# A graph attention layer on one core: prologue loads moved to another queue, more buffers, a score table split in seven

## The chip, the cores and the metric

The kernel runs on one core of one Trainium2 chip. The metric is the device time of one execution in microseconds: 4080.77 in the median of three runs (4079.7 to 4087.65). The profile shown is of one further execution, of 4080.57 us, whose span (from the first to the last profiled instruction) is 4078.8 us.

A core has five engines that run their own instruction streams in order and wait for one another through semaphores: TensorE (PE), VectorE (DVE), ScalarE (ACT), GpSimd (POOL) and SyncE (SP). Data is moved by DMAs, which in this kernel are issued from the streams of SP, ACT and POOL. An engine that waits holds up everything that stands behind the waiting instruction in its own stream.

## The reference

Nodes x (12500 x 64), 400000 edges with a source, a destination and 64 features each; the edges come sorted by destination. For every edge a score is made from its source row, its destination row and its features, a softmax is taken over the edges of one destination, and the weighted source rows and features are summed per destination.

```python
h_src = nfeats[src]
h_dst = nfeats[dst]
z_att = concatenate([h_src, h_dst, efeats])
e = leaky_relu(z_att @ W_attn + b_attn, 0.01)
m = concatenate([h_src, efeats]) @ W_ne
ex = exp(e - segment_max(e, dst)[dst])
alpha = ex / segment_sum(ex, dst)[dst]
z = segment_sum(alpha * m, dst)
out = relu(concatenate([nfeats, z]) @ W_out)
return layernorm(x + out)
```

## The kernel before

**Tiling.** The sorted edges are cut into 782 groups of 512 (128 partitions with four edges each). Groups are handled in chunks of 24 (`sizes`: 32 chunks of 24, then 10, then 4), and inside a chunk in quads of four groups (`SG`). A quad has two buffers: `ze` for its edge features, loaded by one DMA of 512 KB on SP (L143), and `zx` for its source rows, filled by 16 indirect gathers on POOL (L152), one for each group and place. There are ten `ze` and ten `zx` buffers (`ZB`). The indices of a gather are a column of `srcs`.

**Indices.** `indices` (L102) loads a chunk's indices in natural order (`raw`, SP), turns them into floats (`nat`, ACT, L115), transposes them with eight matmuls into `pp` (L118), and casts the sources back to integers (`srcs`, DVE, L121). There is one `raw`, one `nat` and one `pp`, and there are three `srcs`. `slots_of` (L124) makes from the destinations in `pp` and from `d0b`, each group's first destination on all partitions, the relative destinations `drel`.

**Scores.** `scores` (L158) handles one quad: it loads four rows of `wins` (the destination part of the score for the 48 nodes that begin at a group's first destination) on SP, spreads them over the partitions by a matmul (L163), and makes the scores in VectorE from `ze`, `zx` and these rows (L167 to L186). In chunk 0 the gathers read `x` itself and the source part of the score is computed from the rows (L171, L173); in all later chunks they read `table`, which holds x with the source score as a 65th column.

**Softmax and aggregation.** After a chunk's six quads `softmax` (L226) scans the scores of the whole chunk, and `aggregate` (L322) weights them and sums with matmuls (L333) into `pg` and by VectorE into `acc` (L343). A `zx` or `ze` buffer comes free when the matmuls of its quad have read it; only then may POOL and SP fill it for the quad ten further on. `softmax` also needs the neighbouring destinations, `d3`, loaded on SP by `neighbours` (L205).

**The prologue.** Ahead of the loop, the main body (from L357) does the following.
- It converts the first indices and loads `d0i` (every 512th destination, in one row), `d0p` (the same destinations down the partitions, one element per descriptor), the weights `attn`, `b_col`, `wne`, `wout`, all but the indices on ACT's queue.
- It gathers the first quad from x (`ahead`), and makes `d0b` by three matmuls.
- In 14 blocks of seven times 128 nodes it loads x (`xt`, ACT's queue, three buffers, L395), multiplies and sums on VectorE to make each node's source score (into the 65th column of `xt`) and destination score (`sd`; L400 and L403, each twice), and writes the block to `table` (L404, ACT's queue).
- It transposes `sd`, stores it in DRAM as `sdflat` (L412), and lets one DMA on SP copy it 12544 times, shifted by one node each time, into `shifted` (L419).
- Seven indirect gathers on POOL (`wk`, L423, two buffers) pick the rows of `shifted` at the groups' first destinations, and ACT's queue stores each to `wins` (L426). Between `sdflat` and `shifted`, the gathers of the second to fifth quad are written down.

**What sets the order.** The order in which the text names instructions is not the order in which they run: a scheduler places the instructions of each engine by estimated times, and inserts the semaphore waits. Memory pools also give an order: `pre`, which holds `xt`, `prod`, `wk` and others, is closed after the `wk` loop, and `work`, `rows` and `tiny`, opened after it, reuse its memory; their tiles wait for the readers and writers of what stood there. The two clearings of `worst` and `acc` (L430, L431) stand after it and depend on nothing.

Of the kernel before, what the change touches and what calls it, by code (L numbers as in the profile page):

```python
# [9 lines left out]
F32 = mybir.dt.float32  # L10
I32 = mybir.dt.int32
AF = mybir.ActivationFunctionType
# [3 lines left out]
P = 128  # L16
T = 4
GE = P * T
# [7 lines left out]
S = 48  # L26
# [4 lines left out]
EW = 65  # L31
# [8 lines left out]
def sorted_path(ctx, tc, x, dst, idx, edge, w_ne, w_attn, b_attn, w_out, out, flag):  # L40
# [6 lines left out]
    nc = tc.nc  # L47
    N, D = x.shape
    E = edge.shape[0]
    NB = (N + P - 1) // P  # L50
    NFULL = N // P
# [30 lines left out]
    early = dram.tile([NB * P, D], F32, name="early")  # L82
    sdflat = dram.tile([NB * P + S], F32, name="sdflat")
    shifted = dram.tile([NB * P, S], F32, name="shifted")
    wins = dram.tile([NG, S], F32, name="wins")
    d0i = const.tile([1, NG], I32, name="d0i")
    d0b = const.tile([P, NG], F32, name="d0b")
    worst = const.tile([P, 2], F32, name="worst")
# [9 lines left out]
    w_src = fixed[:, S + D:S + 2 * D].unsqueeze(1)  # L98
    alpha = fixed[:, S + 2 * D:S + 2 * D + T * BG].rearrange("p (t g) -> p t g", t=T)
    win = fixed[:, S + 2 * D + T * BG:S + 2 * D + T * BG + SG * S].rearrange("p (g s) -> p g s", g=SG)  # L100

    def indices(g0, G):  # L102

        raw = chunks.tile([BG, P * 2 * T], I32, name="raw", bufs=1)
        if g0 + G < NG:
            nc.sync.dma_start(out=raw[0:G], in_=idx[g0:g0 + G].rearrange("g p c -> g (p c)"))
        else:

            nc.vector.memset(raw, 0)
            if G > 1:  # L110
                nc.sync.dma_start(out=raw[0:G - 1], in_=idx[g0:g0 + G - 1].rearrange("g p c -> g (p c)"))
            nc.sync.dma_start(out=raw[G - 1:G, 0:RP * 2 * T],
                              in_=idx[NG - 1:NG, P - RP:P].rearrange("g p c -> g (p c)"))
        nat = chunks.tile([BG, P * 2 * T], F32, name="nat", bufs=1)
        nc.scalar.activation(nat[0:G], raw[0:G], AF.Copy)  # L115
        pp = psum.tile([P, 2 * T, BG], F32, name="pp", bufs=1)
        for c in range(2 * T):
            nc.tensor.transpose(pp[:, c, 0:G], nat[0:G].rearrange("g (p c) -> g c p", c=2 * T)[:, c, :],  # L118
                                ident[0:G, 0:G])
        srcs = chunks.tile([P, T, BG], I32, name="srcs", bufs=3)  # L120
        nc.vector.tensor_copy(srcs[:, :, 0:G], pp[:, 0:T, 0:G])  # L121
        return srcs, pp

    def slots_of(g0, G, pp):  # L124
# [33 lines left out]
    def scores(g0, n, ze, zx, drel, b0, y, plain):  # L158

        b = g0 - b0  # L160
        wrow = tiny.tile([1, SG, S], F32, name="wrow")
        nc.sync.dma_start(out=wrow[:, 0:n, :], in_=wins[g0:g0 + n, :].unsqueeze(0))
        nc.tensor.matmul(win[:, 0:n, :], ones_row, wrow[:, 0:n, :], start=True, stop=True)  # L163

        yb = y[:, :, b:b + n].rearrange("p t g -> p g t")
        prod = work.tile([P, SG, T, D], F32, name="prod", bufs=1)
        nc.vector.tensor_tensor(prod[:, 0:n], ze[:, 0:n],  # L167
                                w_edge.unsqueeze(1).to_broadcast([P, n, T, D]), op=OP.mult)
# [182 lines left out]
    while left > 0:  # L351
# [3 lines left out]


    prepared = {0: indices(0, sizes[0])}  # L357
    nc.scalar.dma_start(out=d0i, in_=dst.rearrange("(o n) -> o n", o=1)[:, 0:E:GE])
    NW = (NG + P - 1) // P
    d0p = const.tile([P, NW], I32, name="d0p")  # L360
    nc.vector.memset(d0p, 0)
    nc.scalar.dma_start(out=d0p[:, 0:NW - 1], in_=dst[0:(NW - 1) * P * GE].rearrange("(k p e) -> p k e", p=P, e=GE)[:, :, 0])
    nc.scalar.dma_start(out=d0p[0:NG - (NW - 1) * P, NW - 1:NW],
                        in_=dst[(NW - 1) * P * GE:E].rearrange("(e o) -> e o", o=1)[0:E - (NW - 1) * P * GE:GE, :])
    nc.scalar.dma_start(out=attn, in_=w_attn.rearrange("k o -> o k").to_broadcast([P, 3 * D]))
    nc.scalar.dma_start(out=b_col, in_=b_attn.unsqueeze(0).to_broadcast([P, 1]))
    nc.scalar.dma_start(out=wne[0:D, :], in_=w_ne[D:2 * D, :])
    nc.scalar.dma_start(out=wne[D:2 * D, :], in_=w_ne[0:D, :])
    nc.scalar.dma_start(out=wout, in_=w_out.rearrange("(h k) o -> k h o", h=2))
    ahead = [gather(0, min(SG, sizes[0]), prepared[0][0], 0, True)]  # L370


    sd = const.tile([P, NB], F32, name="sd")
    CB = 7
    nc.scalar.activation(fixed[:, 0:S], slots0, AF.Copy)
    nc.scalar.activation(fixed[:, S:S + D], attn[:, 2 * D:3 * D], AF.Copy)
    nc.scalar.activation(fixed[:, S + D:S + 2 * D], attn[:, 0:D], AF.Copy)
    with tc.tile_pool(name="pre", bufs=2) as pre:
        d0f = pre.tile([1, NG], F32, name="d0f", bufs=1)
        nc.vector.tensor_copy(d0f, d0i)  # L380
        for g0 in range(0, NG, 3 * P):
            n = min(3 * P, NG - g0)
            pb = psum.tile([P, 3, P], F32, name="sm").rearrange("p k n -> p (k n)")
            nc.tensor.matmul(pb[:, :n], ones_row, d0f[:, g0:g0 + n], start=True, stop=True)
            nc.scalar.activation(d0b[:, g0:g0 + n], pb[:, :n], AF.Copy)
        for c0 in range(0, NB, CB):
            c1 = min(c0 + CB, NB)
            f1 = min(c1, NFULL)
            n = c1 - c0
            xt = pre.tile([P, CB, EW], F32, name="xt", bufs=3)  # L390
            if c1 > NFULL:
                nc.vector.memset(xt[:, NFULL - c0:NB - c0, :], 0.0)
                nc.scalar.dma_start(out=xt[0:TAIL, NFULL - c0, 0:D], in_=x[NFULL * P:N, :])
            if f1 > c0:
                nc.scalar.dma_start(  # L395
                    out=xt[:, 0:f1 - c0, 0:D],
                    in_=x[c0 * P:f1 * P, :].rearrange("(b p) f -> p b f", p=P))
            for k, to in ((0, xt[:, 0:n, D]), (1, sd[:, c0:c1])):
                prod = pre.tile([P, CB, D], F32, name="prod")
                nc.vector.tensor_tensor(  # L400
# [3 lines left out]
            nc.scalar.dma_start(  # L404
                out=table[c0 * P:c1 * P, :].rearrange("(b p) f -> p b f", p=P),
                in_=xt[:, 0:n, :])
        nc.vector.tensor_scalar(sd, sd, b_col, None, op0=OP.add)
        psd = psum.tile([P, 3, P], F32, name="sm")[0:NB, 0, :]
        nc.tensor.transpose(psd, sd, ident)
        sdt = pre.tile([NB, P], F32, name="sdt", bufs=1)  # L410
        nc.vector.tensor_copy(sdt, psd)
        nc.scalar.dma_start(out=sdflat[0:NB * P].rearrange("(b p) -> b p", p=P), in_=sdt)  # L412
        zero = pre.tile([1, S], F32, name="zero", bufs=1)
        nc.vector.memset(zero, 0.0)
        nc.scalar.dma_start(out=sdflat[NB * P:NB * P + S].unsqueeze(0), in_=zero)
        while len(ahead) < 5 and (len(ahead) + 1) * SG <= sizes[0]:
            ahead.append(gather(len(ahead) * SG, SG, prepared[0][0], 0, True))
        over = sdflat[0:1]
        nc.sync.dma_start(out=shifted, in_=bass.AP(over.tensor, over.offset, [[1, NB * P], [1, S]]))  # L419
        for k in range(NW):  # L420
            m = min(P, NG - k * P)
            wk = pre.tile([P, S], F32, name="wk")
            nc.gpsimd.indirect_dma_start(  # L423
                out=wk, out_offset=None, in_=shifted[:, :],
                in_offset=bass.IndirectOffsetOnAxis(ap=d0p[:, k:k + 1], axis=0))
            nc.scalar.dma_start(out=wins[k * P:k * P + m, :], in_=wk[0:m])  # L426
    work = loop.enter_context(tc.tile_pool(name="work", bufs=2))
    rows = loop.enter_context(tc.tile_pool(name="rows", bufs=1))
    tiny = loop.enter_context(tc.tile_pool(name="tiny", bufs=2))
    nc.vector.memset(worst, 0.0)  # L430
    nc.vector.memset(acc, 0.0)  # L431

    def own_part(c0):

# [572 lines left out]
```

## Time and profile before

| what | value |
|---|---|
| median of three runs | 4080.77 us |
| the profiled execution | 4080.57 us |
| its span | 4078.8 us |
| POOL busy | 2967.8 us (73%), 3142 instructions |
| VectorE busy | 1875.2 us (46%) |
| TensorE matmul busy | 985.2 us (24%) |
| ScalarE busy | 131.6 us (3%) |
| DMA traffic | 239.80 MB, mean 59 GB/s |

Busy is the time in which an engine ran a profiled instruction; issuing a DMA from SP or ACT is not counted as busy, but it occupies that engine's stream, and the timeline lists it (SPq, ACTq).[...] "issue" names idle time of an engine that waited for nothing the profile shows. An average over the whole span hides stages: here the prologue of some 190 us, with nearly no TensorE work, stands ahead of a long regular stretch, and an end of about 100 us follows it. Granted TensorE clock was 1.00 in the first 200 us and 0.55 to 0.60 from 300 to 4000 us.

### The profile page before, as it was taken

Reading aid. Unit: us, or ns where it says so; the run is one execution under the profiler, and the core shown is the slowest. Engines: PE = TensorE matmul, PEld = TensorE weight load, DVE = VectorE, ACT = ScalarE, POOL = GpSimd, SP = SyncE. Lnnn points to the kernel's source line nnn. Section 1 sums busy time; section 2 is a strip of 40 time slices with the busy share of each in tenths; the row PEclk is TensorE's granted clock in tenths of the full one; section 3 lists DMA queues with packets and bytes.
Section 4 is the critical chain, followed back from the end, with each engine's and each line's share of the span. In section 5 each row is a group of like instructions: output and inputs, shape, how many; then the busy total and the mean of one; then the engine's idle time right before and its main releaser. Section 6 shows DMA issues by size and latency. Waiting matters only on the chain.

```text
span 4078.8 us, 40728 instructions
## 1 busy us (share of the span) xinstructions
PE 985.2 (24%) x14494; PEld 766.8 (19%) x14494; DVE 1875.2 (46%) x4448; ACT 131.6 (3%) x287; POOL 2967.8 (73%) x3142
## 2 busy tenths in 40 slices
PE   0022332132222112222212222211222221122235
PEld 0022322122212011111101111211111120111225
DVE  4174443343555443455444355544335544434656
ACT  0000000000000000000000000000000000000001
POOL 6757777777777777777777777777777777777770
PEclk9985665565555555555555555555555555555555
DMA  8122332232222122222212222212222221222214
GB/s 169 29 51 60 75 75 57 46 74 60 60 60 60 28 59 59 59 60 60 48 39 59 59 60 59 60 34 54 59 60 60 60 59 27 59 58 58 55 26 96
DMA packets 315275, 239.80 MB, mean 59 GB/s; under 512 B 160574, under 2 KB 264233, under 8 KB 315062
## 3 DMA queue, kind: packets, MB, share of 16 engines
q0 software_dynamic: 100320, 104.42, 15.6%
q1 hardware_dynamic: 147462, 116.22, 9.6%
q10 hardware_dynamic: 67280, 16.45, 2.0%
q8 instruction: 117, 1.92, 0.2%
q14 instruction: 96, 0.79, 0.1%
HBM read 226.99 MB, written 12.28 MB: 59 GB/s over the span
## 4 chain that ended last, share of the span: by engine, by line
POOL 41%; DVE 22%; issue 17%; PE 11%; DMA 7%; ACT 1%; DVEq 0%; POOLq 0%; ACTq 0%
POOL zx L152 41%; DMA zx<-table,srcs 7%; PE pg L333 5%; DVE prod L167 3%; DVE y L169 3%; DVE prod L181 3%; PE fixed L163 2%; DVE hot L176 2%; PE sm L200 2%; PE sm L192 2%; DVE acc L343 1%; DVE sdst L184 1%; DVE by_row L197 1%; DVE b L273 1%; DVE w L325 1%
## 5 line engine op out<-in xcount | busy, mean ns | idle before, releaser
L152 POOL DMA_INDIRECT zx<-table,srcs x3032 | 2866.8, 946 | 956.7 <-issue 869.6
L163 PE MATMUL fixed<-wrow,ones_row 1*128 1x192 f32 x392 | 179.0, 553 | 2391.3 <-DVE prod L181 2314.5
L121 DVE CAST srcs<-pp 128x96 int32<-128x96 f32 (+2 forms) x34 | 8.6, 253 | 1587.0 <-DMA zx<-table,srcs 1521.5
L163 PEld LDWEIGHTS fixed<-wrow,ones_row 1*128 1x128 f32 x392 | 88.8, 280 | 2464.9 <-DVE prod L181 2385.1
L333 PE MATMUL pg<-w,ze 128*64 128x48 f32 x6256 | 459.3, 244 | 84.3 <-DVE w L325 73.4
L333 PEld LDWEIGHTS pg<-w,ze 128*64 128x64 f32 x6256 | 449.7, 161 | 104.5 <-DVE w L325 90.1
L333 PE MATMUL pg<-w,zx 128*64 128x48 f32 x6256 | 459.5, 244 | 5.3 <-issue 5.0
L333 PEld LDWEIGHTS pg<-w,zx 128*64 128x64 f32 x6256 | 449.7, 161 | 6.0 <-issue 6.0
L167 DVE TENSOR_TENSOR prod<-ze,fixed 128x1024 f32<-128x1024 f32 x196 | 237.6, 1212 | 86.4 <-DMA wins<-wk 49.9
L169 DVE TENSOR_REDUCE y<-prod 128x16 f32<-128x1024 f32 x196 | 237.2, 1210 | 0.0
L343 DVE TENSOR_TENSOR acc<-acc,pg 128x48 f32 x782 | 158.6, 203 | 164.1 <-PE pg L333 112.9
L325 DVE TENSOR_TENSOR w<-hot,fixed 128x768 f32<-128x768 bf16 x196 | 176.8, 944 | 42.9 <-PE pg L333 37.7
L184 DVE TENSOR_REDUCE sdst<-prod 128x16 f32<-128x768 f32 x196 | 186.1, 950 | 5.1
L181 DVE TENSOR_TENSOR prod<-hot,fixed 128x768 f32<-128x768 bf16 x196 | 185.5, 947 | 0.9
L176 DVE TENSOR_TENSOR hot<-fixed,drel 128x768 bf16<-128x768 f32 x196 | 185.9, 948 | 0.0
L115 ACT ACTIVATE nat<-raw 24x1024 f32<-24x1024 int32 (+2 forms) x34 | 35.9, 1056 | 2876.9 <-PE pp L118 2848.2
L152 POOL DMA_INDIRECT zx<-in_x_dram,srcs x96 | 93.5, 974 | 44.2 <-issue 28.7
L200 PE MATMUL sm<-ones_row,by_row 1*128 1x1 f32 x272 | 79.0, 357 | 108.9 <-DVE by_row L197 75.2
L200 PEld LDWEIGHTS sm<-ones_row,by_row 1*128 1x128 f32 x272 | 67.5, 307 | 176.8 <-DVE by_row L197 138.0
L192 PE MATMUL sm<-order,s 128*1 128x128 f32 x136 | 39.8, 396 | 194.6 <-DVE s L258 112.0
L118 PE MATMUL pp<-ident,nat 24*128 24x24 f32 (+2 forms) x272 | 36.3, 279 | 144.2 <-DVE drel L127 111.4
L174 DVE TENSOR_TENSOR y<-y,zx 128x16 f32<-128x16 f32 x196 | 37.0, 189 | 67.5 <-DMA zx<-table,srcs 64.4
(133 smaller groups left out, 1109.2 us busy)
## 6 DMA issues: line engine op xcount, KB each, us to landing
ze<-in_edge_dram SPq DMA_DIRECT2D x194, 512.0 KB
zx<-table,srcs POOLq DMA_INDIRECT x3032
table<-xt ACTq DMA_DIRECT2D x14, 227.5 KB
wrow<-wins SPq DMA_DIRECT2D x195, 0.8 KB
raw<-in_idx_dram SPq DMA_DIRECT2D x32, 96.0 KB
xb<-in_x_dram ACTq DMA_DIRECT2D x24, 128.0 KB
early<-xo ACTq DMA_DIRECT2D x24, 128.0 KB
xb<-in_x_dram ACTq DMA_DIRECT2D x12, 256.0 KB
```

What stands on the lines that cost most here:

```text
L152: nc.gpsimd.indirect_dma_start(out=zx[:, g, t, 0:D] if plain else zx[:, g, t, :], out_offset=None, in_=x[:, :] if plain else table[:, :], ...
L163: nc.tensor.matmul(win[:, 0:n, :], ones_row, wrow[:, 0:n, :], start=True, stop=True)
L167: nc.vector.tensor_tensor(prod[:, 0:n], ze[:, 0:n], w_edge.unsqueeze(1).to_broadcast([P, n, T, D]), op=OP.mult)
L169: nc.vector.tensor_reduce(yb, prod[:, 0:n], axis=AX.X, op=OP.add)
L176: nc.vector.tensor_tensor(hot[:, 0:n], slots.unsqueeze(1).unsqueeze(1).to_broadcast([P, n, T, S]), drel[:, :, b:b + n].rearrange("p t g -> ...
L181: nc.vector.tensor_tensor(at[:, 0:n], hot[:, 0:n], win[:, 0:n].unsqueeze(2).to_broadcast([P, n, T, S]), op=OP.mult)
L184: nc.vector.tensor_reduce(sdst[:, 0:n], at[:, 0:n], axis=AX.X, op=OP.add)
L192: nc.tensor.matmul(p[0:1, :], col, order, start=True, stop=True)
L200: nc.tensor.matmul(p[:, 0:1], by_row, ones_row[:, 0:1], start=True, stop=True)
L325: nc.vector.tensor_tensor(w[:, 0:n], hot[:, 0:n], alpha[:, :, b:b + n].rearrange("p t g -> p g t").unsqueeze(3).to_broadcast([P, n, T, S]) ...
L333: nc.tensor.matmul(pg[at:at + D, g, :], z[:, g, t, 0:D], w[:, g, t, :], start=(t == 0), stop=(t == T - 1))
L343: nc.vector.tensor_tensor(ag, ag, pg[:, g, :], op=OP.add)
```

## The change

All of it is in the prologue.
- `wins` becomes seven DRAM tiles of 128 rows, and the row loads in `scores` pick the tile. `wk` gets seven buffers.
- `attn`, `d0i`, `b_col`, `d0p`, `wne`, `wout` and x are loaded on SP instead of ACT. `d0i` and `b_col` stand after the first x block; `d0p`, `wne` and `wout` are moved down to the place just ahead of `shifted`.
- x gets 14 buffers, and all its loads are written ahead of the compute blocks and of the first gather.
- Everything in the block that computes `table` and `sd` is to be issued after the first cast of sources (`casts[0]`), by `tc.issue_after`; the clearing of `acc` after the copy of the transposed scores (`casts[1]`).
- `d0b` is made after the fourth block of x rather than ahead of the first.

In the order that the scheduler gives the changed kernel, POOL runs 80 gathers from x, then the seven `wk` gathers, then the other 16 gathers from x, then all of those from `table`. ACT's stream begins with the conversion of the first indices. SP's stream begins with the index load, then `attn`, x, `d0i`, `b_col` and the other x blocks, then the first `ze`.

```diff
-    wins = dram.tile([NG, S], F32, name="wins")
+    wins = [dram.tile([P, S], F32, name=f"wins{k}") for k in range((NG + P - 1) // P)]
...
-        nc.vector.tensor_copy(srcs[:, :, 0:G], pp[:, 0:T, 0:G])
+        cast = nc.vector.tensor_copy(srcs[:, :, 0:G], pp[:, 0:T, 0:G])
+        if not casts:
+            casts.append(cast.ins)
...
-        nc.sync.dma_start(out=wrow[:, 0:n, :], in_=wins[g0:g0 + n, :].unsqueeze(0))
+        for k in range(g0 // P, (g0 + n - 1) // P + 1):
+            a, b1 = max(g0, k * P), min(g0 + n, (k + 1) * P)
+            nc.sync.dma_start(out=wrow[:, a - g0:b1 - g0, :], in_=wins[k][a - k * P:b1 - k * P, :].unsqueeze(0))
...
-    nc.scalar.dma_start(out=d0i, in_=dst.rearrange("(o n) -> o n", o=1)[:, 0:E:GE])
...
-    nc.scalar.dma_start(out=d0p[:, 0:NW - 1], in_=dst[0:(NW - 1) * P * GE].rearrange("(k p e) -> p k e", p=P, e=GE)[:, :, 0])
...
-    nc.scalar.dma_start(out=attn, in_=w_attn.rearrange("k o -> o k").to_broadcast([P, 3 * D]))
-    nc.scalar.dma_start(out=b_col, in_=b_attn.unsqueeze(0).to_broadcast([P, 1]))
...
+    nc.sync.dma_start(out=attn, in_=w_attn.rearrange("k o -> o k").to_broadcast([P, 3 * D]))
+    CB = 7
+    before = ExitStack()
+    pre = before.enter_context(tc.tile_pool(name="pre", bufs=2))
+    xts = []
+    for c0 in range(0, NB, CB):
+        c1 = min(c0 + CB, NB)
+        f1 = min(c1, NFULL)
+        xt = pre.tile([P, CB, EW], F32, name="xt", bufs=(NB + CB - 1) // CB)
...
+            nc.sync.dma_start(
+                out=xt[:, 0:f1 - c0, 0:D],
+                in_=x[c0 * P:f1 * P, :].rearrange("(b p) f -> p b f", p=P))
+        xts.append(xt)
+        if c0 == 0:
+            nc.sync.dma_start(out=d0i, in_=dst.rearrange("(o n) -> o n", o=1)[:, 0:E:GE])
+            nc.sync.dma_start(out=b_col, in_=b_attn.unsqueeze(0).to_broadcast([P, 1]))
...
+    with before:
+
+        before.enter_context(tc.issue_after(casts[0]))
...
-            xt = pre.tile([P, CB, EW], F32, name="xt", bufs=3)
...
+            xt = xts[c0 // CB]
...
+            if c0 == 3 * CB:
+                d0f = pre.tile([1, NG], F32, name="d0f", bufs=1)
+                nc.vector.tensor_copy(d0f, d0i)
...
-        nc.vector.tensor_copy(sdt, psd)
+        casts.append(nc.vector.tensor_copy(sdt, psd).ins)
...
+        d0p = pre.tile([P, NW], I32, name="d0p", bufs=1)
...
+        nc.sync.dma_start(out=d0p[:, 0:NW - 1], in_=dst[0:(NW - 1) * P * GE].rearrange("(k p e) -> p k e", p=P, e=GE)[:, :, 0])
...
+        nc.sync.dma_start(out=wout, in_=w_out.rearrange("(h k) o -> k h o", h=2))
         over = sdflat[0:1]
         nc.sync.dma_start(out=shifted, in_=bass.AP(over.tensor, over.offset, [[1, NB * P], [1, S]]))
...
-            wk = pre.tile([P, S], F32, name="wk")
+            wk = pre.tile([P, S], F32, name="wk", bufs=NW)
...
-            nc.scalar.dma_start(out=wins[k * P:k * P + m, :], in_=wk[0:m])
+            nc.scalar.dma_start(out=wins[k][0:m, :], in_=wk[0:m])
...
-    nc.vector.memset(acc, 0.0)
+    with tc.issue_after(casts[1]):
+        nc.vector.memset(acc, 0.0)
```

More of the change, by code (lines that the diff above doesn't have):

```diff
@@ L100, in sorted_path @@
     win = fixed[:, S + 2 * D + T * BG:S + 2 * D + T * BG + SG * S].rearrange("p (g s) -> p g s", g=SG)
+    casts = []
     def indices(g0, G):
@@ L357, in sorted_path @@
     prepared = {0: indices(0, sizes[0])}
-    nc.scalar.dma_start(out=d0i, in_=dst.rearrange("(o n) -> o n", o=1)[:, 0:E:GE])
[L359 to L364, printed above, removed]
-    nc.scalar.dma_start(out=attn, in_=w_attn.rearrange("k o -> o k").to_broadcast([P, 3 * D]))
-    nc.scalar.dma_start(out=b_col, in_=b_attn.unsqueeze(0).to_broadcast([P, 1]))
-    nc.scalar.dma_start(out=wne[0:D, :], in_=w_ne[D:2 * D, :])
-    nc.scalar.dma_start(out=wne[D:2 * D, :], in_=w_ne[0:D, :])
-    nc.scalar.dma_start(out=wout, in_=w_out.rearrange("(h k) o -> k h o", h=2))
+    nc.sync.dma_start(out=attn, in_=w_attn.rearrange("k o -> o k").to_broadcast([P, 3 * D]))
[7 more added lines that the diff above has]
+        xt = pre.tile([P, CB, EW], F32, name="xt", bufs=(NB + CB - 1) // CB)
+        if c1 > NFULL:
+            nc.vector.memset(xt[:, NFULL - c0:NB - c0, :], 0.0)
+            nc.sync.dma_start(out=xt[0:TAIL, NFULL - c0, 0:D], in_=x[NFULL * P:N, :])
+        if f1 > c0:
+            nc.sync.dma_start(
[5 more added lines that the diff above has]
+            nc.sync.dma_start(out=b_col, in_=b_attn.unsqueeze(0).to_broadcast([P, 1]))
     ahead = [gather(0, min(SG, sizes[0]), prepared[0][0], 0, True)]
     sd = const.tile([P, NB], F32, name="sd")
-    CB = 7
     nc.scalar.activation(fixed[:, 0:S], slots0, AF.Copy)
@@ L377, in sorted_path @@
     nc.scalar.activation(fixed[:, S + D:S + 2 * D], attn[:, 0:D], AF.Copy)
[L378 to L385, printed above, removed]
+    with before:
+        before.enter_context(tc.issue_after(casts[0]))
         for c0 in range(0, NB, CB):
             c1 = min(c0 + CB, NB)
-            f1 = min(c1, NFULL)
             n = c1 - c0
-            xt = pre.tile([P, CB, EW], F32, name="xt", bufs=3)
[L391 to L397, printed above, removed]
+            xt = xts[c0 // CB]
             for k, to in ((0, xt[:, 0:n, D]), (1, sd[:, c0:c1])):
@@ L406, in sorted_path @@
                 in_=xt[:, 0:n, :])
+            if c0 == 3 * CB:
+                d0f = pre.tile([1, NG], F32, name="d0f", bufs=1)
+                nc.vector.tensor_copy(d0f, d0i)
+                for g0 in range(0, NG, 3 * P):
+                    n = min(3 * P, NG - g0)
+                    pb = psum.tile([P, 3, P], F32, name="sm").rearrange("p k n -> p (k n)")
+                    nc.tensor.matmul(pb[:, :n], ones_row, d0f[:, g0:g0 + n], start=True, stop=True)
+                    nc.scalar.activation(d0b[:, g0:g0 + n], pb[:, :n], AF.Copy)
         nc.vector.tensor_scalar(sd, sd, b_col, None, op0=OP.add)
@@ L417, in sorted_path @@
             ahead.append(gather(len(ahead) * SG, SG, prepared[0][0], 0, True))
+        NW = (NG + P - 1) // P
+        d0p = pre.tile([P, NW], I32, name="d0p", bufs=1)
+        nc.vector.memset(d0p, 0)
+        nc.sync.dma_start(out=d0p[:, 0:NW - 1], in_=dst[0:(NW - 1) * P * GE].rearrange("(k p e) -> p k e", p=P, e=GE)[:, :, 0])
+        nc.sync.dma_start(out=d0p[0:NG - (NW - 1) * P, NW - 1:NW],
+                          in_=dst[(NW - 1) * P * GE:E].rearrange("(e o) -> e o", o=1)[0:E - (NW - 1) * P * GE:GE, :])
+        nc.sync.dma_start(out=wne[0:D, :], in_=w_ne[D:2 * D, :])
+        nc.sync.dma_start(out=wne[D:2 * D, :], in_=w_ne[0:D, :])
+        nc.sync.dma_start(out=wout, in_=w_out.rearrange("(h k) o -> k h o", h=2))
         over = sdflat[0:1]
```

## The prediction

> **What bounds the kernel now.** I read the busy row first (POOL 73%, DVE 46%, nobody near full), then the chain that ended last (POOL 41%, "issue" 17%), then POOL's own waits, then the timeline of the first 270 us. The first two say that POOL leads, and the waits say what keeps it from working.
>
> ```profile
> L152 POOL DMA_INDIRECT zx<-table,srcs x3032 | 2866.8, 946 | 956.7 <-issue 869.6
> ...
> POOL zx L152 <- issue: 898.3, 2947, 0.3
> POOL zx L152 <- DMA zx<-table,srcs: 33.2, 109, 0.3
> POOL zx L152 <- PE pg L333: 33.2, 2, 32.9
> POOL zx L152 <- DVE srcs L121: 15.2, 1, 15.2
> ```
>
> An indirect gather takes 0.946 us and 0.30 us of issue stand ahead of it each time, so the pace is one per 1.25 us whatever the rest does (2967 steps from 260.67 to 3970.51). There are 96 + 3032 + 7 = 3135 of them: 3919 of 4078.8 us. Only two waits of POOL are longer than 0.3 us: 15.20 us ahead of the first gather and 32.86 us once, for TensorE's aggregation. A change that makes neither shorter is worth nothing; the prologue matters because both lie in it.
>
> ```profile
> 2.15 7.13 ACTq L362 DMA_DIRECT2D d0p<-in_dst_dram  x1
> 3.71 10.52 DVE L431 MEMSET acc<- 128x12548 f32 x1 [2.56 <-issue]
> ...
> 12.55 1.28 ACT L115 ACT_TABLE_LOAD   x1 [12.55 <-DMA d0i<-in_dst_dram]
> ...
> 13.85 1.06 ACT L115 ACTIVATE nat<-raw 24x1024 f32<-24x1024 int32 x1
> ...
> 16.13 0.26 DVE L121 CAST srcs<-pp 128x96 int32<-128x96 f32 x1 [1.77 <-PE pp L118]
> ...
> 16.67 1.15 POOL L152 DMA_INDIRECT zx<-in_x_dram,srcs  x1 [15.20 <-DVE srcs L121]
> ```
>
> This timeline (start us, duration us, engine) shows why the first gather starts at 16.67. ScalarE converts the first indices (L115) only after it has issued six loads, one of which occupies its queue for 7.13 us; VectorE is in the clearing of acc until 14.23. Both end within half a microsecond of each other, so either alone would have held the start. The indices themselves were there long before: bytes of the stretches 1 to 2, 2.0 to 2.2 and 2.2 to 2.4 us (49, 82 and 164 GB/s) add up to 98 KB, which is the whole 24 x 1024 x 4 byte load, and 2.4 to 2.6 moves nothing.
>
> ```profile
> 148.22 0.94 POOL L423 DMA_INDIRECT wk<-shifted,d0p  x1 [0.30 <-issue]
> ...
> 185.68 0.94 POOL L423 DMA_INDIRECT wk<-shifted,d0p  x1 [0.30 <-issue]
> ...
> 191.19 1.22 DVE L167 TENSOR_TENSOR prod<-ze,fixed 128x1024 f32<-128x1024 f32 x1 [49.94 <-DMA wins<-wk]
> ```
>
> ```profile
> 226.87 0.95 POOL L152 DMA_INDIRECT zx<-table,srcs  x1 [0.30 <-issue]
> 260.67 0.94 POOL L152 DMA_INDIRECT zx<-table,srcs  x1 [32.86 <-PE pg L333]
> ```
>
> These are the other wait's cause. Scores (L167) begin at 191.19, after the last of seven wk gathers (185.68) has landed and been stored in wins: prod lies in a pool that reuses the memory of `pre`, where wk stands. From 191.19 it takes 69.5 us to the point where aggregation has read the first of the ten zx buffers (260.67). POOL has filled all ten by 227.8 and stands for 32.86 us. After that it never stands again until its last gather at 3970.51; 107.3 us of tail follow that one's end.
>
> **The change, part by part.**
>
> *First gather.* The ScalarE queue now issues no load before L118 (formerly L115), and acc's clearing waits for the scores' transposed copy (casts[1]). Remaining chain: index load, landed a little after 2.4; I take 2.8 (0.4 for its completion). The table load (1.28, from 0.82) is over at 2.1. Then the same steps as before, 16.67 - 13.85 = 2.82 us from ACTIVATE to gather. First gather at **5.6**. Ends: 2.4 + 2.8 = 5.2; and, if the load shared the DMA engines as the second index load did (issued 14.93, ScalarE waited for it until 20.40: 5.5 us), 0.8 + 5.5 + 2.8 = 9.1. It stands first on SP as it did before, so the row of the first load is nearer. Gain 16.67 - 5.6 = 11.1 us.
>
> A rule speaks against this part. The Trainium skill, "DMA: Bandwidth & Descriptors", section "Issuing engines are not separate DMA queues", says that all issuers share the same 16 DMA engines and that a choice of issuer saves only the issuing time, usually small. Read so, moving loads from ACT to SP gives about nothing and the time would be 4048. The rows above show the issuing time itself as 11.7 us (0.82 to 12.55) in front of a ScalarE instruction that everything waits for. I go by the row; the rule's other half I accept: the bytes before shifted take as long as they did.
>
> *The seven wk gathers.* In the built order of before, POOL runs 96 gathers from x, then 7 from table, 2 wk, 8, 2 wk, 8, 2 wk, 8, 1 wk: the last wk is number 134. After: 80 from x, 7 wk in one run (seven buffers instead of two), 16 from x, then table; the last is number 87. 47 places of 1.25 us are 58.7 us, plus 11.1 of the start: 185.68 - 69.8 = **115.9**. Scores follow 5.5 us later as before (185.68 to 191.19): 121.4. The seven wins tiles by themselves I cost at nothing: before, the first wins row was multiplied (L163) at 153.43, with five wk still to be gathered, so a whole-tile wait was not there to remove.
>
> *The stall.* From scores to release took 69.5 us. Into that stretch now come the neighbour loads and their VectorE work (d3, far, pf and so on, done earlier in before): some fifteen instructions of 0.06 to 0.29, say 3 us, and a wait of 0 to 3 us for the loads, which wait for the same memory. VectorE's cast of the fourth srcs stands behind two score blocks and needs chunk 0's last x gather: 103 gathers end at 5.6 + 103 x 1.28 = 137.4, landed about 140 (2.45); VectorE gets there at 121.4 + 2 x 7.93 + 5 = 142. No wait. Release at 121.4 + 69.5 + 6 = **197**. POOL needs the buffer after 160 + 7 gathers: 5.6 + 167 x 1.25 + 3.0 (the first 96 ran at 1.28 each, 16.67 to 139.5, which I keep) = 217. Twenty microseconds of cover, so 32.56 us (32.86 less the usual 0.30) go. If the cover fails, each microsecond past 217 costs one. Later buffers come free 2.5 us apart and are wanted 20 us apart.
>
> *SP's queue.* Ahead of shifted it now issues 14 x loads and the tail (0.38 and 0.49 each), attn, b_col, d0i (1.29), d0p (7.13 + 0.92), wne twice, wout, and before them all ten ze: about 18 us of added issuing, plus two index loads that wait for ScalarE conversions, and the semaphore waits[...]. What waits behind is shifted, and behind shifted the first wk, on which POOL would stand in order. Work until shifted has landed: The DMA engines are the limit here (busy share 0.7 to 1.2 in nearly every 5 us from 15 to 75). ACT's queue spent 2.0% of the span, 82 us of all 16 engines, on 67280 packets, so the 12,500 rows of x and the 12,544 of table cost 15 us each; ze's 5.2 MB at the 303 GB/s of 5 to 10 us cost 17; shifted took 18 (issued 80.23, traffic falls away at 99); gathers alone, 100 to 140 us, hold a share of 0.14. Laid end to end from 2.5 us: 65 / 0.86 + 2.5 = 78. VectorE needs 14 x 2.12 = 30 us and is done near 40. The d0p issue of 8 us stands in series on SP with the rest of it, and the scores' column (sdflat) waits for conversions 2 and 3: I add up to 15. Shifted lands at 78 to 93; the first wk is due at 5.6 + 80 x 1.28 = **108**. No cost; below 108 it buys nothing either.
>
> *acc's clearing* now runs beside gathers, about 50 to 65 us, hidden by VectorE's wait for wins until 121. The row gives 10.52 us; The Trainium skill, "VectorE: DVE Perf Modes", section "Zero memsets can be issued as uint32 (trn2)", gives one cycle per element, an estimate of 12548 / 0.96 GHz = 13.07 us. The unexplained 2.56 us ahead of the row make up the difference; I take 13.1. What matters is whether it blocks POOL: "SBUF — State Buffer", section "SBUF: two separate sides", warns that a two-port VectorE operation locks GpSimd out of writing gather descriptors. By that, +10.5 to 13.1 us: 4047 to 4050. The nearest row is the memset of d (128x130) at 61.00, inside the gather of 60.55, which took its usual 0.94. I go by the row: 0.
>
> *Nothing else.* Fourteen x buffers remove VectorE's waits for xt (21.1 us in eleven waits) but those lay under POOL's gathers. The order on PE, VectorE and SP from the second or third chunk on is otherwise as it was, and the tail follows POOL.
>
> **Sum.** Against the profiled execution (4080.57, span 4078.8, so 1.77 around it): 4078.8 - 11.1 - 32.6 = 4035.1; + 1.8 = **4037**. The median shown, 4080.77, lies 0.2 above that execution, which is inside the rounding. That is 1.07% less. Its own range is 4033 (start at 5.2, no slow gathers) to 4042 (start at 9.1, a late microsecond or two).
>
> **Rivals.**
> 1. *The stall stays, smaller.* If scores, the neighbour loads or softmax come more than 20 us later than worked out, POOL stands at its 168th gather. With 30 us more: 4047; with none of the stall gone: 4069.5. For: much of what VectorE, SP and ScalarE do in 121 to 145 is newly packed there. Against: the sum of new work is 6 us.
> 2. *POOL stands at the first wk: the slower side.* Before, wk had 49 us of cover (landed 99, wanted 148); after, 15 to 30. From 108 on each microsecond of shifted or d0p costs one, as all later gathers queue behind it in order. Landing at 120 gives 4049; from 152 on the change loses, and at 165, 4037 + 57 = 4094. For: SP now carries a 7.13 us load issue and two ScalarE-dependent loads ahead of shifted, and the scores' path passes through index conversion 2 and 3. Against: even all of it in series is near 105.
> 3. *The start does not move* (indices land late behind nothing that the trace shows, or the first conversion waits for another load): 4048.
> 4. *The clearing locks POOL*: 4047 to 4050.
>
> **Chances.** Forecast 0.74; stall partly or wholly kept 0.09; POOL at wk with shifted landing below 144, 0.05, from 144 to 160, 0.02, later, 0.04; start unmoved 0.02; lock 0.04. What this kernel's measurement can tell from no change I take as 0.2%, 8 us: that is rival 2 with a landing of 144 to 160 (0.02). Only a later one is slower (0.04); all else is faster (0.94). The range leaves out those 0.06, half of rival 1 and the long end of the 0.05 at the top, and a microsecond under my own low end covers the bottom: 4032 to 4050.
>
> **What would show it.** First gather near 5.6; no wait of POOL over 1 us after it, and none at L441; wk in one run near 108 to 117; L174's first prod near 121; the aggregation's first matmul before 200; last gather near 3927; gathers beside acc's clearing still 0.94. A POOL wait for shifted at L441, or for the aggregation near 217, would show me wrong, and its length is the error.

## The result and the profile after

The changed kernel takes 4039.14 us in the median of five runs (4035.9 to 4041.58), against 4080.77 (4079.2 to 4087.65) in five runs of the kernel before: a ratio of 0.9895, with a 95% interval of 0.988 to 0.9909, or 41.6 us less. The profiled execution took 4039.4 us with a span of 4037.6.

The first view is the page of the changed kernel and, below the dots, its table of POOL's instructions by line. The columns are the count, busy us, mean ns of one, and the idle time in front with what ended it.

```profile
span 4037.6 us, 40722 instructions
...
PE 1015.3 (25%) x14494; PEld 792.4 (20%) x14494; DVE 1871.0 (46%) x4448; ACT 131.6 (3%) x287; POOL 2971.0 (74%) x3142
...
L157 POOL DMA_INDIRECT zx<-table,srcs x3032 | 2866.9, 946 | 924.2 <-issue 877.5 <-DMA zx<-table,srcs 25.0 <-PE sm L207 4.6
L157 POOL DMA_INDIRECT zx<-in_x_dram,srcs x96 | 96.8, 1008 | 34.8 <-issue 28.0 <-DVE srcs L124 4.6 <-DMA zx<-in_x_dram,srcs 2.2
L441 POOL DMA_INDIRECT wk<-shifted,d0p x7 | 6.6, 943 | 2.1 <-issue 2.1
```

The amount of work is the same, and so is the length of a gather from table, 946 ns. The idle time of that row fell from 956.7 to 924.2, and "PE pg", the wait for aggregation, is no longer among its releasers. POOL's waits (us in total, times, longest us) say the same:

```profile
POOL zx L157 <- issue: 905.6, 2971, 0.3
POOL zx L157 <- DMA zx<-table,srcs: 25.0, 82, 0.3
POOL zx L157 <- DVE srcs L124: 4.6, 1, 4.6
...
POOL zx L157 <- DMA zx<-in_x_dram,srcs: 2.2, 3, 1.6
```

The wait in front of the first gather is 4.6 us instead of 15.2, the wait of 32.9 is gone, and one wait of 1.6 us, at POOL's 46th gather, for an earlier gather's landing is new. The timeline of the changed kernel shows the same places as were shown of before (start us, duration us, engine):

```profile
3.24 1.05 ACT L118 ACTIVATE nat<-raw 24x1024 f32<-24x1024 int32 x1 [1.14 <-DMA raw<-in_idx_dram]
...
5.52 0.26 DVE L124 CAST srcs<-pp 128x96 int32<-128x96 f32 x1 [3.74 <-PE pp L121]
...
6.06 1.22 POOL L157 DMA_INDIRECT zx<-in_x_dram,srcs  x1 [4.60 <-DVE srcs L124]
...
60.80 0.74 SPq L430 DMA_DIRECT2D d0p<-in_dst_dram  x1
...
63.15 10.52 DVE L450 MEMSET acc<- 128x12548 f32 x1 [2.56 <-issue]
...
74.44 0.55 SPq L437 DMA_DIRECT2D shifted<-sdflat  x1
...
113.41 0.94 POOL L441 DMA_INDIRECT wk<-shifted,d0p  x1 [0.30 <-issue]
...
120.89 0.94 POOL L441 DMA_INDIRECT wk<-shifted,d0p  x1 [0.30 <-issue]
...
126.37 1.18 DVE L174 TENSOR_TENSOR prod<-ze,fixed 128x1024 f32<-128x1024 f32 x1
...
196.17 8.39 SPq L148 DMA_DIRECT2D ze<-in_edge_dram  x5
...
222.26 0.94 POOL L157 DMA_INDIRECT zx<-table,srcs  x1 [0.30 <-PE fixed L170]
...
3931.89 0.94 POOL L157 DMA_INDIRECT zx<-table,srcs  x1 [0.30 <-issue]
```

Read downwards: the conversion of the first indices starts when they land (3.24) and not when ScalarE's queue is through with loads (13.85 before); seven wk gathers in one run; scores at 126.37 instead of 191.19. At 196.17 SP issues the eleventh ze load, which waited for the aggregation's matmuls of the first quad (SP's waits from 190 to 200 name PE pg): the first buffers are free then. POOL wants its eleventh zx at about 222, as its 168th gather, and goes straight on.

### The profile page after: what moved, and what is told of

It reads as the page before. It is cut to its first block, busy times and chain, and to the rows that moved or that the text cites. A ratio compares the mean times of both kernels' runs of the same rounds, so it can differ in the third digit from the quotient of the medians.

```text
span 4037.6 us, 40722 instructions
## 1 busy us (share of the span) xinstructions
PE 1015.3 (25%) x14494; PEld 792.4 (20%) x14494; DVE 1871.0 (46%) x4448; ACT 131.6 (3%) x287; POOL 2971.0 (74%) x3142
## 4 chain that ended last, share of the span: by engine, by line
POOL 42%; DVE 21%; issue 17%; PE 12%; DMA 7%; ACT 1%; DVEq 0%; POOLq 0%; ACTq 0%
POOL zx L157 42%; DMA zx<-table,srcs 6%; PE pg L340 5%; DVE prod L174 3%; DVE y L176 3%; DVE prod L188 3%; PE fixed L170 3%; DVE hot L183 2%; PE sm L207 2%; PE sm L199 2%; DVE sdst L191 1%; PE pg L470 1%; DVE by_row L204 1%; DVE acc L350 1%; DVE b L280 1%
## 5 line engine op out<-in xcount | busy, mean ns | idle before, releaser
L157 POOL DMA_INDIRECT zx<-table,srcs x3032 | 2866.9, 946 | 924.2 <-issue 877.5
L340 PE MATMUL pg<-w,ze 128*64 128x48 f32 x6256 | 474.1, 248 | 82.6 <-DVE w L332 72.6
L340 PEld LDWEIGHTS pg<-w,ze 128*64 128x64 f32 x6256 | 463.4, 165 | 103.5 <-DVE w L332 89.3
L340 PE MATMUL pg<-w,zx 128*64 128x48 f32 x6256 | 474.6, 248 | 7.9 <-issue 7.8
L340 PEld LDWEIGHTS pg<-w,zx 128*64 128x64 f32 x6256 | 463.5, 165 | 9.5 <-issue 9.0
L157 POOL DMA_INDIRECT zx<-in_x_dram,srcs x96 | 96.8, 1008 | 34.8 <-issue 28.0
L121 PEld LDWEIGHTS pp<-ident,nat 24*128 24x128 f32 (+2 forms) x272 | 32.5, 197 | 187.0 <-DVE drel L132 118.4
```

Source lines behind the costliest of these rows:

```text
L157: nc.gpsimd.indirect_dma_start(out=zx[:, g, t, 0:D] if plain else zx[:, g, t, :], out_offset=None, in_=x[:, :] if plain else table[:, :], ...
L340: nc.tensor.matmul(pg[at:at + D, g, :], z[:, g, t, 0:D], w[:, g, t, :], start=(t == 0), stop=(t == T - 1))
```

## The experiments

Each time below is set beside that of the kernel before on the same chip. Three groups (experiments 1 to 4, 5 to 8, and 11) landed on chips on which the kernel before takes 5645 to 5691 us instead of 4081. There, from the main loop on, the engines stand idle with releasers that the profile names "issue" or "remote". Experiments 5 and 12 ran the same kernel, the one on such a chip and the other not. These are TensorE's idle time ahead of the aggregation's matmuls and POOL's waits for them (us in total, times, longest us), the fifth experiment above the dots and the twelfth below:

```profile
PE pg L333 <- issue: 1934.1, 1604, 3.3
POOL zx L152 <- PE pg L333: 1421.2, 83, 39.1
...
PE pg L333 <- issue: 10.4, 14, 2.0
POOL zx L152 <- PE pg L333: 3.1, 2, 2.8
```

POOL is not the bound on the slower chips, so their times say nothing about what the parts are worth where it is. What can be read of these runs is the timeline up to the first scores. Experiments 9, 10 and 12 ran where the kernel before takes 4082 to 4085 us.

### 1 and 2: what holds the first gather

The first experiment leaves the clearing of acc where the scheduler likes to put it:

```diff
-    with tc.issue_after(casts[1]):
-        nc.vector.memset(acc, 0.0)
+    nc.vector.memset(acc, 0.0)
```

> The changed kernel, but the clearing of acc is not put behind the scores' copy, so it stands first on VectorE again. My theory (either of two holds on the first gather is enough to keep it late): the clearing ends at 14.2, the cast of the first sources follows, first gather at 14.9 instead of 6.06, no stall of POOL at its 168th gather, time 4039 + 8.8 = 4048. Rival (the ScalarE queue alone held the start): first gather near 6, time 4039.

First gather at 14.68. ScalarE converted the indices at 2.93, so they and the queue were in time, and the cast still had to stand behind the clearing:

```profile
2.93 1.06 ACT L118 ACTIVATE nat<-raw 24x1024 f32<-24x1024 int32 x1 [0.83 <-DMA raw<-in_idx_dram]
3.64 10.52 DVE L449 MEMSET acc<- 128x12548 f32 x1 [2.56 <-issue]
...
14.16 0.23 DVE L124 CAST srcs<-pp 128x96 int32<-128x96 f32 x1
14.68 1.76 POOL L157 DMA_INDIRECT zx<-in_x_dram,srcs  x1 [13.21 <-DVE srcs L124]
```

The second puts the small loads back on ScalarE's queue, and nothing else:

```diff
-    nc.sync.dma_start(out=attn, in_=w_attn.rearrange("k o -> o k").to_broadcast([P, 3 * D]))
+    nc.scalar.dma_start(out=d0i, ...)
+    nc.scalar.dma_start(out=d0p[:, 0:NW - 1], ...)
+    nc.scalar.dma_start(out=attn, ...)
+    nc.scalar.dma_start(out=wout, ...)
...
```

> The changed kernel, but d0i, d0p, attn, b_col, wne and wout are loaded on ScalarE's queue at their old place; x stays on SP in fourteen buffers. My theory: the conversion of the first indices starts at 13.9 again, first gather at 16.7, no stall at the 168th gather, time 4039 + 10.6 = 4050. Rival, from the rule that the choice of the issuer saves only small issuing time: within 2 us of 4039.

First gather at 14.00, not at 16.7: the six loads held the conversion until 11.18, since d0p's issue took 5.30 us here and not 7.13. Both holds are shown, each alone keeping the start late, by 8.6 and 7.9 us; the size of the second was put 2.7 us too large, 1.8 of it in d0p's issue.

```profile
2.15 5.30 ACTq L369 DMA_DIRECT2D d0p<-in_dst_dram  x1
...
9.89 1.28 ACT L118 ACT_TABLE_LOAD   x1 [9.89 <-DMA d0i<-in_dst_dram]
...
11.18 1.05 ACT L118 ACTIVATE nat<-raw 24x1024 f32<-24x1024 int32 x1
...
14.00 1.22 POOL L157 DMA_INDIRECT zx<-in_x_dram,srcs  x1 [12.53 <-DVE srcs L124]
```

In both runs a late start cost more than its own length. VectorE's multiplications of the x blocks then ran alongside from the first gather on, a pair every 2.1 us without a pause, and the gathers fell in step with them: 14 and 13 of them were long, by 11.4 and 11.2 us in all against 6.2 in the changed kernel (the fourth experiment finds why). The first wk came at 127.48 and 126.11, that is 14.1 and 12.7 us later than the changed kernel's 113.41.

The times were 5687.92 and 5687.68 against 5690.96 (ratios 0.9995, 0.9985 to 1.0005, and 0.9996, 0.9987 to 1.0006) and cannot be used for the sum.

### 3: wins in one tile

```diff
-    wins = [dram.tile([P, S], F32, name=f"wins{k}") for k in range((NG + P - 1) // P)]
+    wins = dram.tile([NG, S], F32, name="wins")
```

> The changed kernel with wins as one DRAM tile again. My theory (the split buys nothing, since the first row was already multiplied before the last wk was gathered): first prod near 126, no stall, 4039 within noise. Rival (a row load waits for all seven stores): same first prod, because prod waits for the last store anyway, but later row loads move; at most 5 us later scores, still inside the cover of 26 us, so the same time; the traces differ in when the first row is multiplied (118.7 against 126 or later).

The first row was multiplied at 117.14, two microseconds before the last wk was even issued (119.34), and the first prod ran at 124.89, where the changed kernel has 126.37. A row load of the single tile waits for the rows it reads and not for the whole; the split buys nothing up to the first scores. Time 5671.55 against 5690.96, ratio 0.9967 (0.9956 to 0.9979).

### 4: the long gathers

The changed kernel's 96 gathers from x are longer on average (1008 ns) than those of before (974 ns). The timeline of the changed kernel, VectorE's multiplications of the x blocks, its cast of `d0i` and POOL's gathers alone, shows which (x2 is two multiplications of some 0.6 us in a row):

```profile
18.33 0.55 DVE L410 CAST d0f<-d0i 1x782 f32<-1x782 int32 x1
18.48 2.29 POOL L157 DMA_INDIRECT zx<-in_x_dram,srcs  x1 [0.31 <-issue]
18.80 1.14 DVE L401 TENSOR_TENSOR prod<-xt,attn 128x448 f32<-128x448 f32 x2
...
22.10 1.21 DVE L401 TENSOR_TENSOR prod<-xt,attn 128x448 f32<-128x448 f32 x2
22.66 0.94 POOL L157 DMA_INDIRECT zx<-in_x_dram,srcs  x1 [0.30 <-issue]
23.91 0.95 POOL L157 DMA_INDIRECT zx<-in_x_dram,srcs  x1 [0.30 <-issue]
24.29 1.15 DVE L401 TENSOR_TENSOR prod<-xt,attn 128x448 f32<-128x448 f32 x2
25.17 1.09 POOL L157 DMA_INDIRECT zx<-in_x_dram,srcs  x1 [0.31 <-issue]
26.42 1.15 DVE L401 TENSOR_TENSOR prod<-xt,attn 128x448 f32<-128x448 f32 x2
26.56 1.82 POOL L157 DMA_INDIRECT zx<-in_x_dram,srcs  x1 [0.30 <-issue]
```

A gather that starts while a multiplication runs ends late by about what is left of that one or of the pair: by 0.15 us at 25.17 and by 0.88 at 26.56. One that had started earlier (23.91) is not touched, nor is the one of 22.66, which started 0.02 us after the second of a pair (22.64). The longest does not fit this alone: it started at 18.48, 0.32 us before its multiplications but inside the cast, whose one operand is in SBUF, and ended 0.8 us after them. Experiments 2, 9 and 10 have the same 2.29 us in the same place. So the cast seems to hold a gather too; no run takes it away alone. The fourth experiment reads the weights from PSUM:

```diff
+    wd = S + 2 * D + T * BG
+    nc.scalar.activation(fixed[:, wd:wd + D], attn[:, D:2 * D], AF.Copy)
...
-            for k, to in ((0, xt[:, 0:n, D]), (1, sd[:, c0:c1])):
+            for at, to in ((S + D, xt[:, 0:n, D]), (wd, sd[:, c0:c1])):
...
-                    attn[:, k * D:(k + 1) * D].unsqueeze(1).to_broadcast([P, n, D]), op=OP.mult)
+                    fixed[:, at:at + D].unsqueeze(1).to_broadcast([P, n, D]), op=OP.mult)
```

> The changed kernel, but the x blocks' weights are read from PSUM (the source weights from where they already stand, the destination weights copied once into the part that win uses later), so that VectorE's multiplications in the prologue have one SBUF input and not two. In the changed kernel fourteen gathers between 6 and 42 us took 1.09 to 2.29 us instead of 0.94, 6.2 us too much in all, each beside such a multiplication, and none after the x blocks are done. Theory A (an SBUF-read conflict between VectorE's two-input multiplications and POOL's gathers): the long gathers go but for the first one, last gather 6 us earlier, 4033. Theory B (loaded DMA engines in the same stretch, or any VectorE work): the long gathers stay, 4039.

Here is the table by line of this kernel, POOL's gathers from x:

```profile
L157 POOL DMA_INDIRECT zx<-in_x_dram,srcs x96 | 91.1, 949 | 34.9 <-issue 29.3 <-DVE srcs L124 4.3 <-DMA zx<-in_x_dram,srcs 1.3
```

The mean falls to 949 ns (1002 in the third experiment, on the same chip with the weights in SBUF). Of the gathers beside the x blocks only the very first is long (1.10), which stays unexplained, and the first wk is issued at 107.64 instead of 113.41. The same loads ran and VectorE did the same multiplications, so neither DMA traffic nor VectorE work as such makes these gathers long: it is the multiplications' second operand in SBUF. Time 5670.31 against 5690.96, ratio 0.9968 (0.9956 to 0.9981).

### 5 and 12: the kernel before with seven wk buffers

```diff
-            wk = pre.tile([P, S], F32, name="wk")
+            wk = pre.tile([P, S], F32, name="wk", bufs=NW)
```

> The kernel before with one thing changed: seven wk buffers instead of two. In the built order the seven wk gathers then stand in one run after 103 others, the last one at place 110 instead of 134. My theory (POOL's order decides when scores begin): first gather 16.7 as before, last wk at 16.7 + 3 + 109 x 1.25 = 156, first prod at 161.5, aggregation has read the first zx at 231, POOL wants it at 228.5: the stall shrinks from 32.9 to 2 or 3 us, time 4051. Rival (the loads on SP or the early x are needed for it): first prod within 10 us of 191, stall over 20, time over 4068.

> The same kernel as the fifth experiment (the kernel before with seven wk buffers), since the chip of that group ran the main loop 1560 us slower and hid the time. Unchanged theory: first prod at 161.6 as seen there, aggregation has read the first zx at 231, POOL wants it at 228.5: a stall of 2 or 3 us instead of 32.9, time 4051. Rival: stall over 20, time over 4068.

In the first of these runs the first prod came at 161.59, and the time (5638.31 against 5644.87, ratio 0.9987, 0.9978 to 0.9997) was covered by the chip's idle time (POOL stood 36.64 us at its 168th gather, since aggregation itself was late). In the second the whole chain can be read:

```profile
156.12 0.94 POOL L423 DMA_INDIRECT wk<-shifted,d0p  x1 [0.30 <-issue]
...
161.56 1.22 DVE L167 TENSOR_TENSOR prod<-ze,fixed 128x1024 f32<-128x1024 f32 x1 [20.01 <-DMA wins<-wk]
...
231.20 0.94 POOL L152 DMA_INDIRECT zx<-table,srcs  x1 [2.84 <-PE pg L333]
```

The stall is 2.84 us instead of 32.86, and the time 4051.24 against 4081.83: ratio 0.9926 (0.9913 to 0.994). This one number of buffers, with none of the moved loads, brings 30.6 of the change's 41.6 us.

### 6 and 7: one hold of the start taken away from the kernel before

```diff
-    nc.vector.memset(acc, 0.0)
+    with tc.issue_after(sdt_copy):
+        nc.vector.memset(acc, 0.0)
```

> The kernel before with only the clearing of acc put behind the scores' copy. My theory: ScalarE's queue still holds the first conversion until 13.9, first gather 16.4 to 16.7; in the built order the last wk moves from place 134 to 137, so scores begin 3.7 us later and the stall grows by as much: 4080.6 + 3.5 = 4084. Rival (the clearing was the hold): first gather before 10, time 4075 or less.

First gather at 16.85, last wk at 189.80 instead of 185.68. The start did not move and the scores came 4.1 us later, at 195.31. Time 5650.74 against 5644.87, ratio 1.001 (1.0001 to 1.002).

The seventh moves the six small loads to SP (`nc.scalar.dma_start` becomes `nc.sync.dma_start` in each).

> The kernel before with only d0i, d0p, attn, b_col, wne and wout moved to SP's queue. My theory: the clearing of acc still holds VectorE until 14.2, first gather at 14.9, the stall stays near 33, time 4079. Rival (the ScalarE queue was the hold): first gather near 6, time 4070.

First gather at 14.75, last wk at 185.69, first prod at 191.35. The gather begins earlier, but the first two took 2.24 and 1.66 us, and by the wk gathers nothing was left of it. Time 5649.26 against 5644.87, ratio 1.0005 (0.9995 to 1.0014). With the first two experiments this shows that the start has two holds and that both must go.

### 8 and 9: less room in x, less in wk

The eighth loads x on SP in the block loop into three buffers (`bufs=3`).

> The changed kernel with x in three buffers again, loaded on SP inside the block loop. In the built order all 96 x gathers and three from table now stand ahead of the seven wk, the last at place 106 instead of 87. My theory (the fourteen buffers only give cover): scores begin 19 x 1.25 = 24 us later, near 150, the aggregation has read the first zx near 220, POOL wants it at 222: no stall or up to 3 us, time 4039 to 4042. Rival (the buffers are what removed the stall): stall over 10 us, time over 4049.

Last wk at 141.29, first prod at 147.19: 20.8 us later than in the changed kernel. Whether POOL then stalls could not be seen, since on this chip aggregation itself was late. Time 5624.46 against 5644.87, ratio 0.9962 (0.9948 to 0.9976).

The ninth takes the changed kernel back to two wk buffers.

> The changed kernel with two wk buffers instead of seven. In the built order the wk gathers come in pairs with eight other gathers between, the last at place 111 instead of 87. My theory: scores begin 30 us later, near 156, the aggregation has read the first zx near 226, POOL wants it at 222: a stall of 3 to 5 us, time 4043. Rival (the run of seven is what removed the stall): stall over 20, time over 4059.

Last wk at 149.78, first prod at 155.45, one wait of POOL:

```profile
225.27 0.94 POOL L157 DMA_INDIRECT zx<-table,srcs  x1 [4.45 <-PE pg L340]
```

A stall of 4.45 us. Time 4048.24 (4043.02 to 4050.39) against 4085.18, ratio 0.9911 (0.9895 to 0.9928): 36.9 us less than before on this chip, where the whole change brings 41.6. The run of seven is thus worth only some 5 us in the changed kernel: the pairs stand between gathers from x, from place 81 on, and end at place 111. What counts is the place of the last wk.

### 10: the slower rival's price

`shifted` is written four times, each after the one before (redundant work, the same contents):

```diff
+        for j in range(3):
+            nc.sync.dma_start(out=shifted, in_=bass.AP(over.tensor, over.offset, [[1, NB * P], [1, S]]))
         nc.sync.dma_start(out=shifted, in_=bass.AP(over.tensor, over.offset, [[1, NB * P], [1, S]]))
```

> The changed kernel with shifted written four times, each after the one before, to make the last of them land late (redundant work, same contents). In the built order 90 x gathers now stand ahead of wk. Price of the slower rival: shifted lands at 94 + 3 x 20 = 154, POOL would be at wk at 127 and stands there 27 us, all later gathers follow as late, no second stall since scores and POOL shift together: 4039 + 27 = 4066. If instead the wait costs nothing (the stall's cover swallows it) the time stays near 4039.

```profile
150.84 0.94 POOL L443 DMA_INDIRECT wk<-shifted,d0p  x1 [26.54 <-DMA shifted<-sdflat]
```

The scheduler puts the first wk at place 91 here and not 81. POOL stands 26.54 us at it and has no second stall. Time 4069.31 against 4085.18, ratio 0.9962 (0.9948 to 0.9976): 15.9 us less than before instead of 41.6. So 25.7 us are lost by a wait of 26.2 over the usual 0.3. The mechanism exists and costs about one for one; the changed kernel only keeps clear of it.

### 11: both remaining costs of the start

The fourth experiment's edit, and the first quad's indices loaded straight into the partitions:

```diff
+    direct = const.tile([P, SG, 2 * T], I32, name="direct")
+    nc.sync.dma_start(out=direct, in_=idx[0:SG].rearrange("g p c -> p g c"))
...
-                at = srcs[:, t, g0 + g - b0:g0 + g - b0 + 1]
+                at = srcs[:, t, g0 + g - b0:g0 + g - b0 + 1] if direct is None else direct[:, g, t:t + 1]
```

> The changed kernel with the x blocks' weights in PSUM, as in the fourth experiment, and with the first quad's indices loaded straight into the partitions (a second small index load, first on SP), so that its 16 gathers need no conversion. Theory: first gather near 3.3 instead of 6.06; all gathers from the second on at 0.94 (6 us less up to the x blocks' end); POOL's last gather 9 us earlier; on a chip where POOL is the bound, 4039 - 9 = 4030. If the engines wait for things the profile cannot name, as on the chips of the first two groups of experiments, the time says nothing and only the first 190 us are read: first gather, lengths of the gathers, first wk near 104.

First gather at 3.07, the gathers from x at 945 and 963 ns, first wk at 106.26, with 81 gathers ahead of it instead of 80 (113.41 in the changed kernel). Time 5621.39 against 5646.96, ratio 0.9956 (0.9941 to 0.997). It was not run on a chip where POOL is the bound. POOL's 81st gather starts at 105.01, 8.4 us ahead of the changed kernel's (113.41), which would put the time near 4031; that is an estimate.

## Why the prediction was right

- **The bound.** POOL's pace and its two waits were the whole story. The 12th experiment takes the second wait away alone and gets its length.
- **First gather** 6.06 for 5.6. The indices were ready for ScalarE at 3.24 and not 2.8; the 2.82 us from there on held (3.24 to 6.06).
- **Last wk** 120.89 for 115.9. The place was right, and the sum's slow gathers were mis-sized: 3.0 us were kept from before, but the x blocks now follow one another closely and more gathers run into a multiplication, 6.2 us of excess (14 gathers of 1.09 to 2.29 us between 6 and 42). With the start's 0.46 and the new wait of 1.6 (1.3 over the usual 0.3) that is the whole 5.0. That this excess comes mainly from VectorE's second SBUF operand was not in the prediction at all: it had put the fourteen x buffers at nothing, since VectorE's waits for x lay under POOL's gathers, but closing those waits lengthened the gathers (mean 1008 ns here, 986 in the eighth experiment with three x buffers). Nor was the wait of 1.6, and the sign "no wait of POOL over 1 us" did not come.
- **First prod and release.** 5.48 us after the last wk as worked out; the first buffer free at about 196 for 197, wanted at 222 for 217. The cover was 26 us, so no stall: right. But 196 for 197 is luck: scores came 5.0 us late, and from scores to release it took 70 us and not 75.5. The 6 us for the neighbour loads and their work were not paid: VectorE reached the end of the scores 48.6 us after the first prod, against 48.0 before.
- **SP's queue.** shifted was issued at 74.44 and traffic fell away at 94, for a landing of 78 to 93: just late of the guess, 19 us ahead of the first wk at 113.41. But the working was off: d0p's issue, put at 8 us in series, took 0.74 and 0.61; the queue was instead held by semaphores. The second index conversion ran only at 58.24, and the third, behind which ACT issues the store of sdflat (69.88), waited until 69.80 for its load; shifted itself waited 4.3 us for that store to land. That dependence is the one that the prediction named.
- **acc's clearing** ran from 63 to 74 beside gathers of 0.94 and 0.95: it does not lock POOL. The row is again 10.52 us with 2.56 unexplained in front of it.
- **The two cancelling sizes.** POOL's last gather was 5 us later than worked out (ends 3932.83 for 3927.8), and the tail 2.6 us shorter (104.8 for 107.3; why stays open). Hence 4037.6 for a span of 4035.1, which is luck in its last 2.5 us. POOL's last gather ended 38.6 us earlier than before: 10.6 of start and 32.6 of stall, less 3.2 of longer gathers and 1.3 of the new wait.
- **The split of wins at nothing**: right by the third experiment. **The fourteen x buffers at nothing of their own**: the scheduler puts wk 19 places later without them, and scores came 20.8 us later in the eighth experiment. That is less than the cover of 26 us, so no stall is to be expected where POOL is the bound; this is an estimate, not measured. Their price in longer gathers is said above.
- **The rule on issuers**: the small loads' issuing time did hold the start (second experiment, 7.9 us), so the row was the right guide; its size differed by run (5.30 and 7.13 for the same d0p load). What the start alone is worth in time was not measured where POOL is the bound; it is read from the timelines.

## What to carry to other kernels

When one engine's count of instructions sets the time, look only at its long waits, and follow each to the place in that engine's own order that decides it: here the place of seven gathers among 3135 was worth 30 us, by one buffer count, and the same count only some 5 us once another edit had moved that place. A late start can have several holds of nearly the same length, as here; list all that end within a microsecond of each other, since removing one of two shows nothing or little. A load placed in front of an in-order gather should have its landing compared with its due time, because past that each microsecond costs about one (the tenth experiment).

## What was not expected of the hardware

- A VectorE multiplication with both operands in SBUF delays an indirect gather that POOL starts while it runs, from 0.94 to as much as 1.82 us, and 2.29 where a cast ran just ahead; with one operand in PSUM it does not (mean 1008 against 949 ns).
- Issuing the same load took very different times: d0p 7.13, 5.30 and 0.74 us, b_col 0.45 and, in the changed kernel at 3.03 us, 3.80.
- Chips differ: the same kernel before took 4081 to 4085 us on some and 5645 to 5691 on others. In the one kernel that ran on both kinds (experiments 12 and 5) VectorE's busy time is equal (1874.2 and 1873.1), while aggregation's matmuls stand idle on "issue" for 10.4 and 1934.1 us. Why stays open.
